# Moving the choice of the processed tokens from the head of the feed-forward to the tail of the attention

## The chip, the cores and the metric

The kernel runs on one core of one Trainium2 chip. A core has five engines that run their own instruction queues in parallel and meet at semaphores: TensorE (PE in the profile, with its weight loads as PEld), VectorE (DVE), ScalarE (ACT), GpSimd (POOL) and SyncE (SP), which here only issues DMAs. The metric is the device time of one execution in microseconds (us), lower is better. The kernel before takes 13212.54 us, the median of three runs.

## The reference, cut to what matters

A Fourier neural operator turns each of 64 images of 256 x 256 into 256 tokens of width 256. 77 text tokens are appended, which makes 333 tokens per image, and one transformer layer follows: attention, then a feed-forward that processes only some of the tokens. This is the part that matters here:

```python
h = jnp.concatenate([h, txt], axis=1)                 # 64 x 333 x 256
h = h + attn(layernorm(h))
h = h + ffn(layernorm(h))

def ffn(x, wr, br, w1, b1, w2, b2):
    weights = (jnp.einsum('bsd,do->bso', x, wr) + br)[..., 0]
    k = max(1, int(0.5 * s))                          # s = 333, k = 166
    kk = k - 1                                        # 165 tokens are kept
    _, idx = jax.lax.top_k(weights, k)
    sel_idx = idx[:, :kk]
    sel = take the rows sel_idx of x
    y = gelu(sel @ w1 + b1) @ w2 + b2
    y = y * weights[sel_idx]
    processed = zeros_like(x), with y put at the rows sel_idx
    return processed + x
```

The 165 tokens with the largest router weights go through the two matrix products (256 to 1024 to 256); all others pass unchanged.

## The kernel before, in words

The first three quarters of the time go to the Fourier layers, whose instruction order is written out by hand (lines up to 705). The change does not touch them. The rest is the transformer stage, one image after another, and there the order on each engine is not the program's: a scheduler of the framework places each instruction on its engine's queue by its own estimate of when its inputs are ready, with the program's order as the preference. On the chip each queue then runs in that fixed order.

For each image b the stage has three parts.

`image_rows(b)` makes the rows of the image. It loads eight pieces `ch` of 1 MB (L829) and adds them up on PE in the PSUM tile `hp` (L831, 32 matmuls), together with a small product of the Fourier modes (L819, L824; their input `a` is made on DVE, L813 and L817). ACT copies the result to `h` (L836), and the text rows come by DMA (L837).

`attention(h)` begins with a layer norm: statistics on DVE (L845, L846), a square root on ACT (L848, tile `ars`), a reciprocal and a scaling on DVE (L849, L853, tile `az`), and transposes on PE (L863). Then come the products for q (L873), the scores (L885), v (L899), transposes of the softmax (L914) and the product of probabilities and v (L923), and the residual sum h1 on DVE (L926). It ends with the second layer norm, of the same kind: `fmv` for the statistics, `frs` for the square root on ACT, and `fz` for the normalized rows that the feed-forward reads.

`feed_forward(b, h1, z)` begins with the choice of the tokens, and it takes no sort. The router weight of each token is a row sum on DVE (L941, `wcol`). To have all weights on every partition, the kernel writes them on the diagonal of a matrix (L945, `dg`) and multiplies by a matrix of ones on PE (L946), which gives `wrow` (L948). For each token DVE counts the weights that are larger (L955, L959, L961, L964); that count is the token's place. A token with a count below 165 is kept, and its weight is noted in `fw` (L965). `place` (L966) is the 0/1 matrix that says which token has which place. For three tiles of up to 128 tokens this is done three times. Then PE gathers the kept tokens with `place` (L973, `zs`) and transposes `place` for the way back (L984, `back`). The two products follow (L990 with a gelu on ACT, L994; L1001, L1005), then transposes (L1011), and the product that puts the rows back (L1020). DVE adds the residual (L1023, after GpSimd has added z to h1 in L1016), and SP stores the rows (L1028).

The loop at the end sets the program's order. It runs one image ahead with the attention, and two ahead with the rows:

```python
    done = attention(hs.pop(0))
    for b in range(B):
        now = done
        if b + 2 < B:
            hs[b + 2] = image_rows(b + 2)
        if b + 1 < B:
            done = attention(hs.pop(b + 1))
        feed_forward(b, *now)
```

Tiles in SBUF named here have two buffers (pool `tt`; `small` has four), so that two images can be in flight. The PSUM tiles `pp` share six buffers, `hp` has two.

ACT needs a table for each kind of function, loaded by an instruction of its own. In this stage it changes three times per image: for exp (L892), for the square root (L848) and for gelu (L994).

## Time and profile before

| What | Value |
|---|---|
| time, median of three runs | 13212.54 us (13204.64 to 13219.62) |
| span of the profiled run | 13202.6 us |
| transformer stage | about 9,950 us to the end |
| PE busy, whole span | 11680.4 us, 88% |
| DVE busy, whole span | 8811.9 us, 67% |
| ACT busy, whole span | 5950.8 us, 45% |
| table loads of ACT in the stage | 64 for exp, 64 for the square root, 63 for gelu, 1283 ns each |

The page divides the span in 40 equal slices and gives the busy share of each engine in tenths. A line of the waits has the engine, tile and line that waited, what it waited for, the sum in us, the number of times and the longest. A line of the timeline has the start and length in us, the engine, the line of the kernel, the operation, the tiles (out <- in), the shapes and the count, and in brackets how long the engine had been idle before and for whom. In the records each matmul of this kernel's float32 data appears as two instructions. PEclk is the granted TensorE clock, 1.00 being full speed.

### The profile page before, as it was taken

The page shows a single profiled execution, that of the slowest core. Times are in us where ns is not written, and L with a number is a line of the kernel's source. Part 1 is how long each engine was busy: PE and PEld are TensorE (multiplying, and loading weights), DVE is VectorE, ACT ScalarE, POOL GpSimd, SP SyncE. Part 2 cuts the span into 40 slices and gives each one's busy share as a digit, 9 for nine tenths or more (in the row PEclk, how much of TensorE's full clock was granted, in tenths as well). Part 3 has the DMA queues.
Part 4 walks back from the last instruction along what each step waited for, and adds up shares of the span by engine and source line. Part 5 has one row for each costly group of instructions (what it writes and reads, how often), then busy time and mean ns, then how long its engine had stood idle before and what let it go on. Part 6 is the DMA issues. An engine that isn't in the chain of part 4 may idle for free.

```text
span 13202.6 us, 406444 instructions
## 1 busy us (share of the span) xinstructions
PE 11680.4 (88%) x182458; PEld 6174.1 (47%) x182458; DVE 8811.9 (67%) x10606; ACT 5950.8 (45%) x9992; POOL 1103.7 (8%) x1183
## 2 busy tenths in 40 slices
PE   6899999997899999999789999999977889898988
PEld 4344444443444444444444444444444656566565
DVE  2777777776777777777677777776765555555554
ACT  2455555554455555555455555555542222222222
POOL 2100000000200000000110000000011100101010
PEclk9899999998999999999999999999998898898988
DMA  4555555555998898899898998888886454545443
GB/s 118 198 204 199 203 204 198 201 205 199 331 350 348 345 354 347 349 352 350 306 342 347 349 352 344 347 346 342 347 306 222 172 192 167 189 176 181 182 174 121
DMA packets 571125, 3484.57 MB, mean 264 GB/s; under 512 B 78225, under 2 KB 129249, under 8 KB 172449
## 3 DMA queue, kind: packets, MB, share of 16 engines
q1 hardware_dynamic: 565376, 3454.84, 69.6%
q8 instruction: 1428, 23.40, 0.7%
q0 software_dynamic: 4000, 3.71, 0.1%
q14 instruction: 321, 2.62, 0.1%
HBM read 1761.32 MB, written 1696.92 MB: 262 GB/s over the span
## 4 chain that ended last, share of the span: by engine, by line
PE 71%; DVE 17%; issue 7%; DMA 4%; ACT 1%; POOL 1%; SPq 0%; DVEq 0%; ACTq 0%; POOLq 0%
PE ring L607 14%; PE ring L624 13%; PE ring L572 10%; PE ring L583 7%; PE ring L647 4%; PE hp L831 3%; PE pp L990 3%; DVE t L595 3%; DVE vo L591 2%; DVE zt L634 2%; PE pp L1001 2%; PE pp L923 2%; PE pp L1020 2%; PE pp L885 2%; PE pp L899 1%
## 5 line engine op out<-in xcount | busy, mean ns | idle before, releaser
L595 DVE STREAM_TRANSPOSE t<-vo 128x2048 f32<-128x2048 f32 x1536 | 3550.1, 2311 | 174.0 <-ACT vo L590 13.8
L614 ACT ACTIVATE ring<-ring 128x1024 f32<-128x1024 f32 x3072 | 3108.8, 1012 | 1190.8 <-PE ring L607 1155.2
L607 PE MATMUL ring<-vo,w 32*32 32x512 f32 x49152 | 2850.9, 622 | 388.5 <-DVE zt L634 139.3
L590 ACT ACTIVATE vo<-ring 128x1024 f32<-128x1024 f32 x1536 | 1569.7, 1022 | 3011.2 <-PE ring L583 2363.7
L591 DVE TENSOR_SCALAR vo<-ring 128x1024 f32<-128x1024 f32 x1536 | 1859.4, 1211 | 594.5 <-PE ring L583 405.5
L624 PE MATMUL ring<-t,cst 32*32 32x512 f32 x49152 | 1864.0, 602 | 299.1 <-issue 298.6
L634 DVE STREAM_TRANSPOSE zt<-ring 128x1024 f32<-128x1024 f32 x384 | 711.9, 1925 | 1645.7 <-PE ring L624 1645.7
L607 PEld LDWEIGHTS ring<-vo,w 32*32 32x32 f32 x49152 | 761.4, 104 | 1894.2 <-ACT ring L614 487.2
L624 PEld LDWEIGHTS ring<-t,cst 32*32 32x32 f32 x49152 | 976.0, 103 | 1146.9 <-issue 694.3
L583 PE MATMUL ring<-vin,ws 32*32 32x512 f32 x32768 | 1230.9, 604 | 18.1 <-issue 13.7
L542 POOL TENSOR_TENSOR ams<-am,sk 48x512 f32<-48x512 f32 x384 | 486.8, 1268 | 8437.0 <-DMA am<-mix 7913.3
L647 PEld LDWEIGHTS ring<-cst,zt 128*128 128x128 f32 x4608 | 534.3, 193 | 176.6 <-ACT vo L590 163.3
L614 ACT ACTIVATION_READ_ACCUMULATOR ring<-ring 128x1 f32 x3072 | 584.2, 190 | 0.0
L647 PE MATMUL ring<-cst,zt 128*128 128x96 f32 x4608 | 566.4, 280 | 10.1 <-DVE zt L634 9.2
L831 PE MATMUL hp<-ch,win 128*32 128x512 f32 x4096 | 527.3, 634 | 5.3 <-DMA ch<-v 5.3
L973 PE MATMUL pp<-place,fz 128*128 128x165 f32 (+1 forms) x768 | 243.0, 475 | 291.6 <-DVE place L966 276.1
L553 PE MATMUL ring<-ams,cst 49*128 49x512 f32 (+1 forms) x1536 | 391.7, 620 | 59.4 <-POOL ams L542 49.0
L583 PEld LDWEIGHTS ring<-vin,ws 32*32 32x32 f32 x32768 | 252.8, 103 | 398.5 <-issue 367.3
L890 DVE TENSOR_REDUCE mx<-pp 128x1 f32<-128x333 f32 (+1 forms) x192 | 96.5, 503 | 507.6 <-PE pp L885 504.0
L990 PE MATMUL pp<-zs,w 128*128 128x165 f32 x2048 | 382.2, 356 | 0.4
L1016 POOL TENSOR_TENSOR h<-h,fz 128x256 f32<-128x256 f32 (+1 forms) x192 | 172.6, 924 | 2509.2 <-DVE fz L853 2509.2
L990 PEld LDWEIGHTS pp<-zs,w 128*128 128x128 f32 x2048 | 371.3, 233 | 4.3 <-DVE zs L163 3.8
(955 smaller groups left out, 12155.0 us busy)
## 6 DMA issues: line engine op xcount, KB each, us to landing
v<-vo SPq DMA_DIRECT2D x1536, 1024.0 KB
vin<-v SPq DMA_DIRECT2D x1024, 1024.0 KB
ch<-v SPq DMA_DIRECT2D x512, 1024.0 KB
mix<-ob SPq DMA_DIRECT2D x192, 256.0 KB
am<-mix SPq DMA_DIRECT2D x384, 96.0 KB
xin<-in_x_dram SPq DMA_DIRECT2D x64, 256.0 KB
mv<-in_x_dram SPq DMA_DIRECT2D x256, 64.0 KB
out_dram<-o SPq DMA_DIRECT2D x1024, 16.0 KB
```

The lines of the kernel that those rows point to most:

```text
L572: nc.tensor.matmul(ps[n][:, 256 * r:256 * r + 256], lhsT=y_[b][32 * n:32 * n + K, t // 4, q:q + 4, :].rearrange("p q c -> p (q c)"), rhs=m ...
L583: nc.tensor.matmul(ps[n][32 * j:32 * j + 32], lhsT=ws[32 * n:32 * n + 32], rhs=v[32 * n:32 * n + 32, 2 * j:2 * j + 2, :], start=False, sto ...
L590: nc.scalar.activation(of[:, 0:2], t2[0], AF.Relu)
L591: nc.vector.tensor_scalar(of[:, 2:4], t2[1], 0.0, None, ALU.max)
L595: nc.vector.transpose(t32[b, t // 2][:, :, 8 * (t % 2):8 * (t % 2) + 8, :].rearrange("p y s c -> p s y c"), o.rearrange("p s (y l) -> p s ...
L607: nc.tensor.matmul(ps[n][32 * j:32 * j + 32], lhsT=w4[i + 1][32 * n:32 * n + 32], rhs=o[32 * n:32 * n + 32, 2 * j:2 * j + 2, :], start=Tru ...
L614: nc.scalar.activation(t2[n], t2[n], AF.Square, accum_out=acc[:, at:at + 1])
L624: nc.tensor.matmul(ps[n][32 * j:32 * j + 32], lhsT=FYT[32 * n:32 * n + 32, k, :], rhs=t32[b, j][32 * n:32 * n + 32, k].rearrange("p s c -> ...
L634: nc.vector.transpose(zt[:, h].rearrange("p k c -> p c k"), t2[h].rearrange("p n (s c) -> p c (n s)", c=C),)
L647: nc.tensor.matmul(ps[:, 0, 96 * g:96 * g + 96], lhsT=zt[:, h, k0:k0 + 4, :].rearrange("p k c -> p (k c)"), rhs=FX[:, h, 48 * r:48 * r + 9 ...
L831: nc.tensor.matmul(hp[32 * g:32 * g + 32], lhsT=win[:, 7 - t:39 - t], rhs=ch[:, g], start=False, stop=t == 7, skip_group_check=True,)
L990: nc.tensor.matmul(ps[:, :KEPT], lhsT=w1[:, dh, 128 * hb:128 * hb + 128], rhs=zs[:, dh, :], start=dh == 0, stop=dh == 1,)
```

## The change

The code that chooses the tokens (from `wcol` to `place`, L936 to L966) is taken out of `feed_forward` unchanged and becomes a function `select(z)`, which returns `fw` and `place`. `attention` now calls it at its end, and hands its results on with h1 and z. In program order the choice for image b+1 therefore stands ahead of the feed-forward of image b, instead of behind it, and ahead of the rows and the attention of the images after. The aim is that `place` exists when the feed-forward begins. No operation is added or left out.

```diff
-        return h1, layer_norm(h1, "f")
-
-    kept = [slice(0, 128), slice(128, KEPT)]
-
-    def feed_forward(b, h1, z):
+    def select(z):
         wcol = small.tile([128, 3], F32, name="wcol")
         ps = psum()
...
             nc.vector.tensor_scalar(place[:r, t, :], IOTA[:r], gt[:r], None, ALU.is_equal)
+        return fw, place
+
+    def attention(h):
+        z, zT = layer_norm(h, "a")
...
+        z = layer_norm(h1, "f")
+        return (h1, z) + select(z)
+
+    kept = [slice(0, 128), slice(128, KEPT)]
+
+    def feed_forward(b, h1, z, fw, place):
         zs = tp.tile([128, 2, KEPT], F32, name="zs")
```

Because the order on the engines is the scheduler's, the diff alone does not tell how the queues change. In the built program a steady image differs from before in this. On PE the first two L946 matmuls stand after the last eight hp matmuls (L831), right ahead of the gathering L973, the third among L973, and all three belong to the image whose attention has just ended, while L973 belongs to the image before. On DVE all of the selection follows `fz` in one piece, with the statistics of the next image's first layer norm spread among it and ended behind it. On ACT the square root `ars` of that layer norm, which stood ahead of the gelus, stands between the seventh and the eighth gelu, and so there are 315 table loads in the program instead of 193.

## The prediction

> **What bounds the kernel now.** I read the page's slices first, to find the stage that the change touches. The last quarter of the span, from about 9,950 us on, is the image-by-image transformer; all before it is untouched.

> ```profile
> PE   6899999997899999999789999999977889898988
> DVE  2777777776777777777677777776765555555554
> PEclk9899999998999999999999999999998898898988
> ```

> There TensorE (PE) is nearly full, VectorE (DVE) half full, and the granted TensorE clock is below that of the slices before. So PE sets the pace: a gain must come from its waits or its clock. Next I asked for the waits of that stage.

> ```profile
> PE pp L973 <- DVE place L966: 276.1, 64, 5.5
> PE pp L1020 <- DVE ys L163: 25.3, 62, 0.4
> PE pp L1011 <- ACT yT L1005: 17.4, 64, 0.3
> ```

> One wait matters: once per image PE waits for the selection matrix `place`. PE's timeline of one image shows where:

> ```profile
> 11586.36 2.00 PE L923 MATMUL pp<-v,probT 77*128 77x256 f32 x8
> 11588.19 0.61 PE L946 MATMUL pp<-dg,cst 128*128 128x128 f32 x4
> 11588.73 1.06 PE L831 MATMUL hp<-ch,win 128*32 128x512 f32 x8
> 11589.73 0.45 PE L946 MATMUL pp<-dg,cst 77*128 77x77 f32 x2
> 11590.10 1.06 PE L831 MATMUL hp<-ch,win 128*32 128x512 f32 x8
> 11595.59 2.47 PE L973 MATMUL pp<-place,fz 128*128 128x165 f32 x8 [4.42 <-DVE place L966]
> ```

> The scheduler had already drawn half of the selection forward: L946 uses a `dg` made one image earlier. Only the comparisons after it (wrow to place) end in the 4.42 us hole. Last I cut the same image, and one about 85 us earlier, into stretches of 3.41 us (columns: stretch, length, busy time and count of PE, PEld, DVE, ACT, POOL, then clock, DMA share, GB/s):

> ```profile
> 11592.63:11596.04 3.41, 0.45 (x3) 0.48 (x4) 3.41 (x12) 0.00 (x0) 2.72 (x3) 1.00 1.01 394
> 11596.04:11599.45 3.41, 3.31 (x13) 2.39 (x12) 3.41 (x20) 0.30 (x1) 0.00 (x0) 0.50 0.45 138
> 11599.45:11602.86 3.41, 3.41 (x15) 3.37 (x15) 2.87 (x10) 2.26 (x4) 0.99 (x2) 0.50 0.02 5
> 11602.86:11606.28 3.42, 3.42 (x26) 3.42 (x26) 1.58 (x5) 2.50 (x7) 1.26 (x2) 1.00 0.00 0
> ...
> 11507.29:11510.70 3.41, 2.73 (x11) 1.36 (x10) 0.91 (x2) 0.59 (x2) 0.00 (x0) 1.00 0.00 0
> 11510.70:11514.11 3.41, 3.41 (x8) 0.84 (x6) 0.96 (x2) 0.00 (x0) 0.00 (x0) 0.50 0.13 24
> ```

> A stretch with little PE work is followed by whole stretches at half clock. The hole costs twice: its length, and slow matmuls after it. The second pair shows another trigger, the thin end of the feed-forward (L1011, L1020), which fires in about one image of four.

> **The budget of one image.** L990 starts at 10443.08 and, 23 images later, at 11600.53: 50.32 us each. PE idle in it: 4.42 + 0.27 + 0.41 = 5.1 us. The half-clock spells of four successive images, read off the clock in steps of 1 us, last 3.42 + 10.24 (the thin end) + 10.24 + 6.82 + 10.24 = 40.96 us, so 10.24 per image; some 0.36 of that is idle anyway, and half of the rest is lost: 4.94 us. What is left, 50.32 - 5.10 - 4.94 = 40.3 us, is PE work at full clock. The change leaves it alone.

> [...] everything queued behind L973 waits with it. [...] `place` takes 0.29 us alone and up to 0.67 us, `dg` 0.26 and up to 0.85, beside GpSimd's adds. [...]

> **The change, part by part.** Nothing is added to the arithmetic. In the built order the steady image differs in three places.

> *1. The wait on place goes.* Selection for image b+1 now completes while image b is in its feed-forward, so L973 finds `place` one image old. Removed: 4.42 us.

> *2. A new wait stands on PE a little earlier.* The two ones-times-`dg` matmuls (L946) of image b+1 now stand right after the eight hp matmuls (L831), ahead of L973. Being in order, they hold up L973, the transposes L984 and all of the feed-forward. Take the end of the attention's last product as 0. DVE: residual add starts at 0.5 and takes 0.48, statistics 0.43, aggregate 0.18 (1.6); ACT's square root 0.30, handovers 0.1 to 0.2, reciprocal 0.17 (2.2); the three L853 fz operations 1.46 (3.6); two L941 weight sums at 0.41 (4.4); first `dg` 0.26: 4.65. But GpSimd's adds h1+z (L1016, 2.72 us for three) start 0.55 us after fz, beside L941 and `dg`. Before, they made the five DVE operations from 11544.05 to 11545.96 last 1.9 us where these alone take 1.1. I add the same 0.85: `dg` at 5.5. Bounds: 4.65 with no contention; 6.5 if all 2.72 us go first (2.75 + 2.72 + 0.82 + 0.26). PE has 2.1 us of hp work (8 matmuls, 1.06 per four), then stalls until 5.6: 3.5 us (2.6 to 4.5).

> *3. ACT's square root for the next layer norm falls between the 7th and 8th gelu.* DVE now has the whole selection ahead of these statistics. That adds two table loads per image (sqrt in, gelu back). ACT after the 7th gelu: 1.28 + 0.30 + 1.28 + 0.40 = 3.26 us. The 7th gelu ends about when L990 ends, and PE then has eleven L1001 matmuls that don't need the 8th, at 303 ns or less (32 records in 4.67 us with overlap, so 0.28 each): 3.1 us. With DVE's statistics done near 15.5, where the sqrt load ends at about 15.3, the stall is some 0.4 us (0.2 to 2, if DVE is later). The rest of the loads lies beside L1001.

> The back eviction, moved behind the comparisons on DVE, is due only after seven L1001 matmuls; az, ys, o, GpSimd and the DMA queue keep slack (DVE idles over 7 us ahead of ys; DMA share 0.50). Moved names cost nothing.

> *4. The clock.* [...] Before, the spells after the hole average (3.42 + 10.24 + 6.82 + 10.24) / 4 = 7.7 us. The hole is shorter, so I take 0.9 times two windows, 6.1 us, and keep 10.24 / 4 = 2.6 us for the thin end: 8.7, less 0.5 idle, half lost: 4.1 us (1 to 6). This term is the least certain.

> Sum: 40.3 + 3.5 + 0.7 + 0.4 + 4.1 = 49.0 us against 50.3, 1.3 us per image. 62 images are in this state: about 80 us. 13212 - 82 = 13130 us. First and last image add a few us either way.

> **The rivals.** *The clock recovers.* Without contention the stall is 2.6 us, and may split between two windows so that neither fires. Idle 3.7, clock loss about 1: 45.0 us, 5.3 less, 330 us in all: 12,880 us. For it: windows with 1.96 us of PE work (11589.21) did not fire. Against: GpSimd starts in the same place. *A wash.* The new stall with its half-clock spell costs what the old one did; 50.0 to 50.6 us, 13,190 to 13,235 us. For it: 3.5 and 4.42 are near, and spells come in whole windows. *Slower.* Full contention (stall 4.5), ACT late by 1.5 us, and the longer idle makes the thin end fire more often: 40.3 + 4.5 + 0.7 + 1.5 + 4.9 = 51.9 us, 1.6 more per image: 13,310 us; with 0.9 more 13,270. For it: the table loads and L1001's wait are new, close to the thin end. Against: the L1001 margin is 3.1 of 3.26 us.

> **How the numbers follow.** Modest gain 0.54, clock recovers 0.14, wash 0.11, slower 0.21. The point is the first's 13,130. The range 12,930 to 13,290 leaves out most of the second case and the far end of the slower one, about 0.1 each. Faster by over 0.2% (26 us) is the first two: 0.68; same 0.11; slower 0.21.

> **What would show it.** Right: L973's wait on `place` gone; a wait of about 3.5 us at the ones-times-`dg` matmuls on `dg`; 64 more sqrt and gelu loads; a wait of about 0.4 us at L1001 on gelu; clock near 0.9 in this stage. Wrong: a `dg` wait of over 4.4 or under 2.6 us, an L1001 wait of over 1 us, or half-clock time per image far from 8.7 us.

## The result, and the profile after

The changed kernel takes 12901.4 us (12889.5 to 12918.6) against 13212.2 us before: ratio 0.9766, interval 0.9749 to 0.9783. It is faster by 311 us, nearly four times the 82 us of the forecast, and lies below the forecast range; the rival "the clock recovers" (12,880 us) is the case that came.

The slices of the page, changed kernel:

```profile
PE   7799999999699999999969999999996899999998
PEclk9899999999899999999989999999997999999999
```

In the last nine slices, all in the transformer stage, the granted clock now reads 9 throughout, where six of the nine read 8. Finer, over the 500 us from 11,400 us on: mean clock 0.90 before, 0.99 after. The waits of the whole span:

```profile
PE pp L880 <- DVE dg L879: 197.3, 64, 7.6
...
PE pp L1005 <- ACT g L998: 3.6, 24, 0.2
```

The wait on `place` (276.1 us) is gone, and the wait on `dg` has taken its place. The lines are shifted by the move: L880 is the ones-times-`dg` product (L946 before), L977 the gathering (L973), L1005 the second product (L1001). The timeline of one image on PE, and DVE's `dg`:

```profile
11537.63 1.92 PE L831 MATMUL hp<-ch,win 128*32 128x512 f32 x16
...
11541.61 1.42 DVE L879 TENSOR_SCALAR dg<-cst,wcol 128x128 f32<-128x128 f32 x2
11542.49 1.08 PE L880 MATMUL pp<-dg,cst 128*128 128x128 f32 x4 [2.94 <-DVE dg L879]
11543.41 0.73 PE L977 MATMUL pp<-place,fz 128*128 128x165 f32 x4
```

```profile
11538.10:11541.51 3.41, 1.45 (x16) 0.24 (x8) 2.94 (x10) 0.98 (x2) 1.42 (x2) 1.00 1.00 375
11541.51:11544.93 3.42, 2.31 (x15) 2.10 (x16) 3.28 (x12) 0.00 (x0) 1.43 (x2) 1.00 1.00 424
...
11582.48:11585.89 3.41, 1.39 (x16) 0.18 (x8) 2.94 (x10) 0.98 (x2) 1.48 (x2) 1.00 0.99 370
...
11626.85:11630.26 3.41, 1.34 (x16) 0.13 (x4) 2.94 (x12) 0.98 (x2) 1.53 (x2) 1.00 0.96 356
11630.26:11633.67 3.41, 2.54 (x10) 2.46 (x11) 2.65 (x10) 0.00 (x0) 1.32 (x2) 0.50 1.01 425
11633.67:11637.09 3.42, 3.42 (x16) 3.32 (x16) 3.03 (x13) 0.30 (x1) 0.00 (x0) 0.50 0.48 107
```

In the first image an edge of the windows, at 11541.51, lies inside the stall: 1.96 us of idle fall in one window and 1 us in the next, and both keep the full clock. One image later the first of the two windows holds 1.39 us of PE work instead of 1.45 and keeps the clock too. Two images later, with the edge slid by 0.1 us in all, it holds 1.34 us, and two windows at half clock follow.

In the 2,160 us from 10,400 us on there are 13 such spells, 64.9 us in all: 1.4 us per image, where it was 10.1. All 13 stand behind the stall at `dg`. In the kernel before, 43 spells behind the hole took 7.5 us per image, and 11 at the thin end of the feed-forward took 2.6. After the change the thin end has none, though nothing was done there.

Measured from one L819 to the next, an image takes 44.85 us on average (50.24 before), and an image without half clock 44.31 to 44.33 us. That is where the time went: 5.4 us per image over the steady stretch, which alone would be 334 us for 62 images; the spans differ by 315. By the prediction's budget some 4.4 of the 5.4 us are clock (a loss of 4.94 became 0.53) and 1.1 are waits (the stall shorter by 1.48 us, less 0.41 for ACT); the experiments ask how far that split holds.

### The profile page after: what moved, and what is told of

It reads as the page before. It is cut to its first block, busy times and chain, and to the rows that moved or that the text cites. A ratio compares the mean times of both kernels' runs of the same rounds, so it can differ in the third digit from the quotient of the medians.

```text
span 12887.7 us, 406626 instructions
## 1 busy us (share of the span) xinstructions
PE 11449.8 (89%) x182458; PEld 6025.9 (47%) x182458; DVE 8775.7 (68%) x10606; ACT 6088.1 (47%) x10114; POOL 1110.9 (9%) x1183
## 4 chain that ended last, share of the span: by engine, by line
PE 69%; DVE 16%; issue 7%; DMA 4%; ACT 3%; POOL 1%; SPq 0%; DVEq 0%; ACTq 0%; POOLq 0%
PE ring L607 14%; PE ring L624 13%; PE ring L572 11%; PE ring L583 7%; PE ring L647 4%; PE hp L831 3%; DVE t L595 3%; DVE vo L591 2%; DVE zt L634 2%; PE pp L959 2%; PE pp L994 2%; PE pp L1024 2%; PE pp L921 2%; PE pp L935 1%; PE pp L909 1%
## 5 line engine op out<-in xcount | busy, mean ns | idle before, releaser
L583 PE MATMUL ring<-vin,ws 32*32 32x512 f32 x32768 | 1240.2, 608 | 19.9 <-issue 17.4
L831 PE MATMUL hp<-ch,win 128*32 128x512 f32 x4096 | 487.1, 604 | 5.1 <-DMA ch<-v 5.1
L1020 POOL TENSOR_TENSOR h<-h,fz 128x256 f32<-128x256 f32 (+1 forms) x192 | 182.5, 975 | 1886.6 <-DVE fz L853 1886.6
L1005 PE MATMUL pp<-g,w 128*128 128x165 f32 x2048 | 314.8, 306 | 9.2 <-ACT g L998 3.6
L994 PE MATMUL pp<-zs,w 128*128 128x165 f32 x2048 | 305.4, 307 | 3.3 <-DVE zs L163 3.3
L1005 PEld LDWEIGHTS pp<-g,w 128*128 128x128 f32 x2048 | 292.2, 189 | 24.4 <-ACT g L998 24.4
```

What stands on the lines that cost most here:

```text
L583: nc.tensor.matmul(ps[n][32 * j:32 * j + 32], lhsT=ws[32 * n:32 * n + 32], rhs=v[32 * n:32 * n + 32, 2 * j:2 * j + 2, :], start=False, sto ...
L831: nc.tensor.matmul(hp[32 * g:32 * g + 32], lhsT=win[:, 7 - t:39 - t], rhs=ch[:, g], start=False, stop=t == 7, skip_group_check=True,)
L1005: nc.tensor.matmul(ps[:, :KEPT], lhsT=w2[:, hb, 128 * dh:128 * dh + 128], rhs=g[:, hb, :], start=hb == 0, stop=hb == HID // 128 - 1,)
```

## The experiments

Ten kernels were run, beside the kernel before (13,215 to 13,221 us in those runs). "Quiet" is an image without half clock, given where at least five images of the stretch are quiet; the half clock per image is the length of all spells between 10,400 and 12,560 us over the number of images.

| Kernel | Time (us) | Wait at dg (us) | Image, mean (quiet) | Half clock per image |
|---|---|---|---|---|
| before | 13212.2 | none; 4.42 at place | 50.24 | 10.1 |
| after | 12901.4 | 2.94 | 44.85 (44.32) | 1.4 |
| b_fill | 13080.4 | none; 3.5 in four pieces | 48.16 (47.42) | 1.9 |
| a_long1 | 13155.7 | 4.15 | 49.47 | 10.2 |
| a_long3 | 13174.9 | 5.61 | 50.06 | 10.1 |
| a_shift | 13016.6 | 2.94 | 47.10 | 5.5 |
| a_nopool | 12899.6 | 2.07 | 44.87 (42.98) | 3.9 |
| a_fillz | 12876.3 | 0.54 + 1.38 | 45.04 (44.32) | 1.5 |
| a_gather_act | 12853.8 | 1.70 | 44.70 | 4.1 |
| a_gather_frs | 12792.2 | 1.26 | 43.90 (42.32) | 3.2 |
| a_gather_all | 12872.4 | 0.45 | 45.43 | 6.1 |
| a_gather_all_fill | 12717.5 | 0.45 | 42.54 | 0 |

Two theories on the 311 us stood against each other. W: the time is that of the wait removed, less that of the new one. C: most of it is the clock. Some expectations put figures on a window: half clock follows it when it holds less than some 1.4 us of work, or more than 2.0 us of idle time, and so always at a stall of over 4.04 us. These are estimates of mine from the rows above: 1.39 us of work, 2.02 us idle, kept the full clock, and 1.34 us of work lost it; not every window below follows them.

**b_fill: the clock of the kernel before, alone.** Work that nobody reads is put into its hole.

```diff
         nc.vector.tensor_scalar(wrow, ps[:, :TOK], brB, None, ALU.add)
+        for _ in range(8):
+            nc.tensor.matmul(ps[:, 384:512], lhsT=ONES, rhs=ONES, start=True, stop=True)
```

> The kernel before, with eight matmuls of ones by ones (128 columns each) per image put into the stall ahead of the gathering matmuls; their results go to unused columns of the weight row's PSUM tile and are read by nobody. The stall's length and every other instruction stay. Theory C (the clock is the larger part of the gain: a 3.41 us window with under about 1.4 us of PE work halves the clock): no window of the stall is thin any more, so an image takes 40.3 + 5.1 + up to 1.3 us instead of 50.3, and the kernel 12890 to 12960 us. Theory W (the shorter wait itself made the gain, the clock follows something else): the extra PE work gains nothing, 13190 to 13260 us.

Measured: 13080.4 us, ratio 0.9891 (0.9876 to 0.9906). The half clock did go, from 10.1 to 1.9 us per image, but only 2.1 of the 5.4 us per image came with it. PE's timeline tells why:

```profile
11537.83 1.60 PE L950 MATMUL pp<-cst 128*128 128x128 f32 x12 [0.66 <-DVE wrow L948]
11542.58 0.80 PE L975 MATMUL pp<-place,fz 128*128 128x165 f32 x4 [1.52 <-DVE place L968]
...
11546.00 0.83 PE L975 MATMUL pp<-place,fz 77*128 77x165 f32 x4 [1.15 <-DVE place L968]
```

With the gathering at full clock, PE now also waits for the second and third tile of `place`. In the kernel before these waits were covered: while DVE made the third tile, PE was busy with the first two at half clock. From the start of `wrow` to the third gathering it is 8.8 us in both kernels (11590.21 to 11599.01 in the kernel before, 11537.20 to 11546.00 here): DVE's chain sets this stretch, and the full clock shows only behind it, where the first product (L992) takes 4.76 us and had taken 5.85 and 6.98 in two images of the kernel before. So the half clock there cost less than half its length, and clearing it pays fully only when the wait for `place` is gone too. Neither theory holds alone.

**a_long1 and a_long3: the new stall made longer.** The first weight sum is made twice, or four times.

```diff
-            nc.vector.scalar_tensor_tensor(
-                junk[:r, :D], z[:r, t, :], 1.0, wrB[:r], ALU.mult, ALU.mult, accum_out=wcol[:r, t:t + 1]
-            )
+            for _ in range(2 if t == 0 else 1):
+                nc.vector.scalar_tensor_tensor(
+                    junk[:r, :D], z[:r, t, :], 1.0, wrB[:r], ALU.mult, ALU.mult, accum_out=wcol[:r, t:t + 1]
+                )
```

> The changed kernel with the first router-weight sum done twice, which makes the wait for dg 0.4 us longer: 3.35 us instead of 2.94. Theory C with the windows' phase: the part of the stall on either side of a window's edge may be at most 2.0 us, which leaves 0.7 us of the 3.41 us for a quiet position instead of 1.1, and the image no longer lasts nearly 13 windows; half-clock spells come back in more than half of the images, 46 to 48.5 us per image, 12970 to 13130 us. Theory W: 0.41 us by 62 images, 12925 us.

> The changed kernel with the first router-weight sum done four times: the wait for dg is 1.23 us longer, 4.17 us. Theory C: a stall of over 4.04 us has no quiet position, so every image has a half-clock spell; 48.5 to 50.5 us per image, 13130 to 13260 us, all of the gain gone though the wait is still shorter than before. Theory W: 1.23 us by 62 images, 12977 us.

Measured: 13155.7 us (ratio 0.9948, 0.9933 to 0.9963) and 13174.9 us (0.9959, 0.9945 to 0.9973). The first step was larger than meant, since the third weight sum moved ahead of `dg` in DVE's queue and was stretched to 0.93 us beside GpSimd:

```profile
11526.40 1.20 PE L881 MATMUL pp<-dg,cst 128*128 128x128 f32 x4 [4.15 <-DVE dg L880]
```

The time of a_long1 is above its interval, that of a_long3 inside, both with a longer stall than expected. Still they separate the theories: 1.21 us more of stall cost 4.62 us per image, 254 us in all, and 1.46 us more after that (5.61 us) only 0.6 us per image. W would give 75 us for the first step. So C holds for the changed kernel: with half clock in every image nearly the whole gain is lost.

The stall didn't do this alone. In a_long1 the spells behind the stall last 222 us over the stretch. Those at the thin end last 225 us, in every second image; the edit doesn't touch it, and the changed kernel has no spell there. So the two runs show that the loss doesn't grow in step with the stall, but not that 2.94 us lies below a border of length.

**a_shift: is 2.94 us below a threshold, or does it lie well?**

```diff
             ps = psum()
             for dh in range(2):
                 nc.tensor.matmul(
                     ps[:, :TOK], lhsT=wqk[:, dh, 128 * eh:128 * eh + 128], rhs=zT[:, dh, :],
                     start=dh == 0, stop=dh == 1,
                 )
+            nc.tensor.matmul(ps[:, 384:512], lhsT=ONES, rhs=ONES, start=True, stop=True)
```

> The changed kernel with two more matmuls of ones by ones (128 columns) per image beside the q products, into columns of the PSUM tile that nobody reads: about 0.55 us more PE work per image, far from the stall. It asks whether the changed kernel is quick because an image of 44.32 us is 0.06 us short of 13 windows of 3.413 us, so that a window edge stays inside the stall for image after image. Theory L (lock): the stall stays at 2.9 us, but an image of about 44.9 us slides by 0.5 us against the windows, the edge leaves the stall and most images get a half-clock spell: 46.0 to 47.5 us per image, 12,970 to 13,070 us. Theory T (a stall under 3 us is simply tolerated): only the added work is paid, 62 x 0.55 = 34 us: 12,925 to 12,945 us.

Measured: 13016.6 us, ratio 0.9858 (0.9841 to 0.9874); theory L. The added work is about 0.6 us (four records; sixteen of the same kind took 2.3 us in b_fill), the stall is 2.94 us as before, and no image of the stretch is without half clock. (One group of hp products also moved, by one product of probabilities and v.) The windows at one stall:

```profile
11648.85:11652.26 3.41, 0.47 (x6) 0.07 (x1) 3.17 (x10) 0.85 (x2) 2.44 (x3) 1.00 0.87 322
11652.26:11655.67 3.41, 3.41 (x13) 3.25 (x14) 2.30 (x8) 0.00 (x0) 0.41 (x1) 0.50 1.01 404
```

Here the whole stall falls in one window. A quiet image of the changed kernel, 44.32 us, is 0.06 us short of 13 windows of 3.413 us (44.37), so the edge that cuts its stall moves by only 0.06 us per image and stays in the stall for six images of eight. Its good clock rests in part on this near match: the small insertion, far from the stall, gave 115 us of the 311 back, of which its own length is some 36.

The image lengths show more. For most of the stretch they repeat in a cycle that fills a whole number of windows: in the changed kernel 8 images (six of 44.32 us, one of 46.85, one of 45.64), 358.4 us or 105 windows; in the kernel before 4 images, 201.4 us or 59 windows; in a_shift 5 images, 235.5 us or 69 windows; in a_long1 2 images, 99.0 us or 29 windows. So the alignments that occur are not a fair sample: each loop settles into a few of them. That the spells do this, since they begin at a window's edge and lengthen the image they fall in, is likely and not shown.

**a_fillz: the stall cut in two by work.** In `select`, ahead of the weight sums:

```diff
+        for _ in range(4):
+            nc.tensor.matmul(ps[:, 384:512], lhsT=z[:, 0, 0:128], rhs=ONES, start=True, stop=True)
```

> The changed kernel with four more matmuls (fz of the first token tile by ones, 128 columns), placed between the hp matmuls and the ones-times-dg matmuls. They become ready when fz is written, about 2 us ahead of dg, so they take no time from anything but cut the stall of 2.94 us in two pieces of 0.5 to 1.5 us with about 1 us of work between. Theory C (the 0.68 us per image that the changed kernel still loses to half clock come from this stall): no half-clock spell is left behind the stall, every image takes about 44.3 us, 12,860 to 12,880 us. Rival (the spells left come from other places, as the thin end of the feed-forward): spells stay, 12,895 to 12,910 us.

Measured: 12876.3 us, ratio 0.9747 (0.9732 to 0.9761), where the changed kernel has 0.9766 (0.9749 to 0.9783). The time is in the interval foreseen, but the two intervals overlap, so a gain isn't shown, and the trace doesn't bear the reason out: 12 spells of 71.7 us remain, nine of them behind the stall after windows with 1.6 to 2.0 us of PE work, three at the thin end. So this run settles nothing on the 1.4 us that are left. It shows that busy time alone doesn't decide: windows with 1.45 us of hp work kept the full clock, and these with 1.64 us of ones-times-`dg` and like products lost it.

**a_nopool: the contention with GpSimd.** The line in which GpSimd adds z to h1 is left out.

> The changed kernel without GpSimd's additions of z to h1 (so the last residual leaves out z). It measures what the contention between GpSimd and VectorE adds to the new stall. My prediction put 0.85 us on it. If that holds, the stall at dg falls from 2.94 to 2.0 to 2.2 us, no window is idle enough for half clock, and an image takes 43.3 to 43.6 us: 12,800 to 12,830 us. Rival (the stretched dg beside GpSimd is chance, and the chain is as long without it): stall 2.8 to 2.94 us, 12,880 to 12,905 us.

DVE's `fz` in the changed kernel, and `fz`, `dg` and the stall without the addition:

```profile
11539.53 1.46 DVE L853 TENSOR_SCALAR fz<-h,fmv,frs 128x256 f32<-128x256 f32 x3
...
11617.79 1.05 DVE L853 TENSOR_SCALAR fz<-h,fmv,frs 128x256 f32<-128x256 f32 x3
11619.45 0.47 DVE L879 TENSOR_SCALAR dg<-cst,wcol 128x128 f32<-128x128 f32 x2
11619.88 1.09 PE L880 MATMUL pp<-dg,cst 128*128 128x128 f32 x4 [2.07 <-DVE dg L879]
```

`fz` takes 1.05 us instead of 1.46, two `dg` take 0.47 instead of 1.42, and the stall is 2.07 instead of 2.94: the contention costs 0.87 us of stall. From the start of `fz` to the start of `dg` it is 0.42 us, from there to the product 0.45. The runs show that these operations take longer beside GpSimd's, not by what means. But the time, 12899.6 us (0.9771, 0.9753 to 0.9788), is that of the changed kernel; I had expected 70 to 100 us less. The windows show what took it:

```profile
11616.59:11620.00 3.41, 1.34 (x13) 0.28 (x6) 2.98 (x13) 0.98 (x2) 0.00 (x0) 1.00 0.98 360
11620.00:11623.41 3.41, 3.41 (x15) 3.41 (x16) 2.12 (x9) 0.00 (x0) 0.00 (x0) 0.50 1.00 419
```

A stall of 2.07 us that lies whole in a window leaves 1.34 us of work there, and a window at half clock follows. A quiet image became 1.34 us shorter (42.98; besides the stall, the product L880 no longer waits for the second `dg` and takes 0.68 us instead of 1.08), and so no longer near 13 windows. In most images the shorter stall lies inside one window or the thin end gets a spell of 10.24 us. For most of the stretch the cycle is 6 images in 78 windows, 44.37 us each: all of the gain went back into the clock.

**a_gather_act, a_gather_frs: real work in the stall.** The gathering of image b doesn't need the choice of image b+1, but stands behind it on PE. In these versions it stands ahead of it, with its copies on ACT.

```diff
+        zs, back = gather(z, place)
+        if b + 1 < B:
+            done += select(done[1])
+        feed_forward(b, h1, z, fw, zs, back)
```

> The changed kernel with the gathering of the kept tokens (matmuls with place, transposes of place, and their evictions, all on ScalarE) put ahead of the next image's choice in program order, so that this PE work fills the wait for dg. Theory C: the wait at dg falls to about 0.4 us and no spell follows it; a wait of up to 1.5 us may come at the transposes of the feed-forward's result, behind the square root on ScalarE; 42 to 44 us per image, 12720 to 12850 us. Theory W: 2.5 us less wait, 1.5 us of it given back, about 12840 us. Both expect a gain; the number of half-clock spells tells them apart: none after dg by C.

Measured: 12853.8 us, ratio 0.9717 (0.9702 to 0.9731). The stall is still 1.7 us, because on ACT the square root `frs`, which `dg` waits for, came to stand behind the copy of `zs`:

```profile
12407.82 0.30 ACT L980 COPY zs<-pp 128x165 f32<-128x165 f32 x1 [5.73 <-PE pp L976]
12408.14 1.28 ACT L848 ACT_TABLE_LOAD   x1
12409.43 0.30 ACT L848 ACTIVATE frs<-fmv,epsc 128x3 f32<-128x3 f32 x1
12409.76 0.17 DVE L849 RECIPROCAL frs<-frs 128x3 f32<-128x3 f32 x1 [1.62 <-ACT frs L848]
```

The time is just above C's interval and near W's 12,840, and 43 spells behind the stall speak against C's "none". Most images have one of them and last 44.36 to 44.40 us, 13 windows again.

In the next version the copies of `zs` take a bias of zero that is made from `frs`, so they can't be queued ahead of it.

```diff
+            zero = small.tile([128, 1], F32, name="zero")
+            nc.scalar.mul(zero, rs[:, 0:1], 0.0)
...
+            nc.scalar.activation(zs[:, dh, :], zps[dh][:, :KEPT], AF.Identity, bias=zero, scale=1.0)
```

> A version meant to beat both: the six gathering matmuls of image b stand ahead of the choice for image b+1 in program order, and their results are copied to zs on ScalarE with a bias of zero that is made from frs of image b+1, so that the copies can't stand ahead of the square root in ScalarE's queue as they did in the version before. PE then has hp, 3.7 us of gathering and again hp in the time in which VectorE makes dg. If the stall is what is left of the loss, it falls from 2.94 to 0 to 0.8 us, there is no half clock behind it, and an image takes 41.7 to 42.8 us: 12,705 to 12,775 us. Rival (another wait takes its place, as ScalarE's square root did): 44 us or more per image, 12,850 us or more.

Measured: 12792.2 us, ratio 0.9683 (0.9667 to 0.9699). It beats both kernels, but by less than expected. The stall is 1.26 us: I had taken the gathering at 3.7 us from rows of the kernel before that ran at half clock, and at full clock it is 1.85. And 3.2 us of half clock per image remain, behind the stall and at the thin end.

**a_gather_all, a_gather_all_fill: the other trigger.** The first also puts the transposes of `place` ahead of the choice. The second adds three matmuls in the feed-forward's wait for `ys`.

```diff
+            if c == 1:
+                for _ in range(3):
+                    nc.tensor.matmul(ps[:, 384:512], lhsT=yT[:, 1, 0:128], rhs=ONES, start=True, stop=True)
             evict(ys[:n, c, :], ps[:n, :D], 2)
```

> The version with the gathering ahead of the choice, and now also the transposes of place (for back) ahead of it, all four copies on ScalarE behind frs. They are 0.9 us of PE work, so the stall at dg should fall from the 1.26 us of that version to 0.3 to 0.5 us. Theory F (a filled stall is a gain twice): no half clock behind it, quiet images of 41.4 to 41.6 us, the thin end of the feed-forward keeps firing as in that version (10.24 us of half clock in one image of four): 12,680 to 12,740 us. Rival G (given back, as when GpSimd's additions were left out: the shorter image locks on the windows at another place and the thin end fires more often): 12,780 us or more.

> The same with three more matmuls (yT by ones, 128 columns) behind the transposes of yT, in the wait for ys, so that the thin end of the feed-forward holds more PE work. If the half clock after the thin end comes from too little PE work in a window there, it goes, and the time falls by another 0.5 to 1.3 us per image against the version without the three matmuls, 30 to 80 us less than that. If what counts there is something else (the transposes and the products with 37 rows that stand in that window are busy time too), the spells stay and the three matmuls cost 0 to 0.5 us per image: 0 to 31 us more.

Measured: 12872.4 us (0.9737, 0.9721 to 0.9753) and 12717.5 us (0.9619, 0.9605 to 0.9634). The first has its stall down to 0.45 us, and yet is 80 us slower than the version with 1.26 us of stall. That is the time of rival G, but not all of its reason. The waits of an image got no shorter, they moved: at the thin end PE now waits 0.97 us for `yT` and 0.59 for `ys`, where it was 0.27 and 0.41. The loss is in the clock, 2.9 us more of half clock per image: no spell is left behind the stall, but there are 24 at the thin end in 47 images, where a_gather_frs had 8. The windows there:

```profile
12308.67:12312.08 3.41, 1.96 (x7) 1.03 (x8) 2.04 (x8) 0.95 (x3) 2.09 (x3) 1.00 0.00 0
12312.08:12315.49 3.41, 3.41 (x8) 1.20 (x7) 0.81 (x2) 0.00 (x0) 0.09 (x1) 0.50 0.03 4
...
12322.32:12325.73 3.41, 3.41 (x20) 0.79 (x16) 0.00 (x0) 0.00 (x0) 0.00 (x0) 0.50 0.69 238
```

The two windows left out read 0.50 too, with PE busy all through: it gets the full clock back only after the fourth. With the three matmuls the same place reads, in PE's timeline:

```profile
12236.29 0.44 PE L1026 MATMUL pp<-cst,yT 128*128 128x128 f32 x2 [0.97 <-ACT yT L1020]
12236.56 0.83 PE L1029 MATMUL pp<-cst,yT 128*128 128x128 f32 x6
12237.31 3.75 PE L1038 MATMUL pp<-ys,back 128*128 128x256 f32 x12
```

They fill the wait of 0.59 us and add a little, and not one half-clock spell is left in 2,100 us: 155 us saved by work that nobody reads, where 30 to 80 were expected. A lucky alignment isn't the reason. A steady image lasts 42.59 us, 12.48 windows, so that the images of the stretch start at all places of a window, in steps of at most 0.2 us, and at none does a window hold less than 2.4 us of PE work. This is the fastest version, 495 us below the kernel before.

## Why the prediction was wrong, point by point

*The order and the two waits: right.* The wait on `place` went, and a wait on `dg` came where it was foreseen.

*Step 2, the new stall: 3.5 foreseen, 2.94 measured, inside its bounds.* From the end of the attention's last product (11537.70) to the first ones-times-`dg` product it is 4.79 us and not 5.6; the hp work ends after 1.85 us and not 2.1. Two errors make the 0.8 us. The contention of 0.85 us looks right beside the 0.87 of a_nopool, but that is luck: 0.42 of the 0.87 lie in `fz`, which the prediction had already taken at its stretched 1.46 us, so about 0.4 was counted twice. And lengths were added, but DVE's operations overlap; two weight sums of 0.41 us start 0.34 us apart.

*Step 3, ACT's detour through the square root: right.* Table loads are 125 for the square root and 124 for gelu, where 64 and 63 had been. In ACT's timeline the eighth gelu stands behind two loads and `ars`, and in PE's the second product takes 5.08 us in every image, where it had taken 4.67:

```profile
11550.50 5.08 PE L1005 MATMUL pp<-g,w 128*128 128x165 f32 x32
11550.56 1.28 ACT L848 ACT_TABLE_LOAD   x1
11551.85 0.30 ACT L848 ACTIVATE ars<-amv,epsc 128x3 f32<-128x3 f32 x1
11552.17 1.28 ACT L998 ACT_TABLE_LOAD   x1
11553.46 0.40 ACT L998 ACTIVATE g<-pp,b1c 128x165 f32<-128x165 f32 x1
```

The loads take the 1.28 us that the forecast put on each, and the next instruction starts 0.01 us behind them. The 0.41 us are the 0.4 of the forecast. The waits show only a fraction as PE's own (the line of L1005 above): most of it falls on the weight loads, inside the group, which wait 24.4 us for `g` over the 64 images.

*Step 4, the clock: this step failed.* It put the half clock at 8.7 us per image, 6.1 behind the stall and 2.6 at the thin end, and the loss at 4.1 us. Measured are 1.4 us behind the stall, none at the thin end, and a loss of 0.53 us (44.85 less 44.32). All else in the sum holds: a quiet image of 44.32 us less 2.94 for the stall, 0.68 for the two short waits and 0.41 for ACT leaves 40.3 us of PE work, as taken. Of the 4.15 us between the sum of 49.0 and the 44.85 measured, the stall makes 0.56 and the clock 3.57. Three things were wrong in it.

First, the step took nearly every stall of 3.5 us to be followed by half clock (its factor of 0.9), an estimate of mine that no run had shown. In the changed kernel windows with 1.39 us of hp work, 2.02 us idle, kept the full clock, and in 12 of the 13 spells 2.04 us or more of the 2.94 lay in one window. (The 13th, at 12531.38, follows a window with 1.95 us of ones-times-`dg` and gathering work, so idle time is not the whole measure.) The kernel before could not test this: around its hole, windows with 1.95 us of work or more kept the full clock and those with 0.45 us or less lost it, and none lay between.

Second, alignment was treated as spread evenly. With 2.04 us as the border, a stall of 2.94 us would be quiet in a third of all alignments, an estimate ((2 x 2.04 - 2.94) / 3.41). In the changed kernel 34 of 47 images are quiet, in a_shift, with the same stall, none. The loop keeps to a few alignments (the cycles above), and nothing in the change aims at good ones; that they came out well is in part luck.

Third, the 2.6 us of the thin end were carried over from the kernel before, without a reason why they would stay. The thin end itself is the same, with waits of 0.27 and 0.41 us in both kernels, but its 11 spells became none; in a_long1, which leaves it alone too, there are 22.

*The budget.* It took the idle time and the half-clock loss of the kernel before as two terms that add. b_fill shows that they covered each other in part. The error doesn't show in the forecast, since both terms were removed or replaced together.

*The rivals.* "The clock recovers" named the right case (a stall split between two windows, as at 11541.51) and the right time, but tied it to a stall of 2.6 us. A stall of 4.5 us, the slower rival, was near what a_long1 had (4.15): that run took 13,156 us, so with a stall near that length a small gain was left.

What stays open: which measure of activity decides. Neither busy time nor idle time orders all the windows: hp products with 1.39 us passed, `dg` products with 1.64 us didn't, the thin end fails with 2.7 us of transposes and of products of which half have 37 rows, and with the three matmuls in it a window with 2.42 us passes. No run measured this by itself. The four executions of the changed kernel lie within 29 us of each other, but it was not tried whether another build keeps the alignment.

## What to carry to other kernels

Where a loop has a stall of the length of those here (2.07 to 4.42 us) on TensorE, don't price the stall alone: read from the clock of the trace whether its half-clock spells lie on a grid, as they do here at 3.413 us, see how the grid cuts the stall, and compare the loop's period with a whole number of windows; here a remainder of 0.06 us kept a good cut for six images of eight. Then find the number of rounds after which the lengths repeat. A change that shortens a stall or adds work elsewhere moves the cut, and that can cost as much as it saves, or more than its own length: in a_nopool 0.87 us less of stall gained nothing, in a_shift 0.6 us of work per image cost 115 us. What removed the half clock here was PE work in each low stretch, real work first: in a_gather_all_fill no window holds less than 2.4 us of it, and no spell is left in 2,100 us, though the images start at all places of a window.

## What the runs showed of the hardware

A gap of 2.07 us on PE that lay inside one window was followed by half clock (a_nopool, 1.34 us of work in the window), while one of 2.94 us that an edge cut in two was followed by none in 34 of 47 images of the changed kernel.

The way back took from one to four windows. Behind the stall at `dg` of the changed kernel it was one in seven spells and two in six, at the thin end three or four (10.2 us in all 11 spells of the kernel before, 10.2 or 13.7 us in a_gather_all), in the rows of a_gather_all with PE busy all the time.
